# A two-layer relational GNN on one NeuronCore: the list of unseen edges built in smaller pieces

## The chip, the cores and the metric

One core of one Trainium2 chip. The metric is the device time of one execution in microseconds (us). The core has five engines that run side by side, each with its own queue of instructions in a fixed order: TensorE (PE, matmuls into the PSUM banks), VectorE (DVE), ScalarE (ACT), GpSimd (POOL, which issues the gathers) and SyncE (SP, which issues the other DMAs). They wait for one another through semaphores.

## The reference

A graph of 12,500 nodes with 128 features and 200,000 edges sorted by target. Every edge has one of 10 relations (the argmax of ten of its attributes). A layer averages the source features by target and relation, multiplies each average with the relation's matrix, and adds a root term and a bias. Two layers, a residual and a layer norm:

```python
def _rgcn_layer(x, src, dst, edge_type, w_rel, root, bias):
    seg = dst * NUM_REL + edge_type
    sums = segment_sum(x[src], seg, N * NUM_REL)
    cnt = segment_sum(ones, seg, N * NUM_REL)
    mean = (sums / maximum(cnt, 1.0)[:, None]).reshape(N, NUM_REL, -1)
    return einsum('nrd,rdo->no', mean, w_rel) + x @ root + bias

h = relu(_rgcn_layer(x, ..., w_rel1, root1, b1))
out = layernorm(x + _rgcn_layer(h, ..., w_rel2, root2, b2))
```

## The kernel before

A tile is 128 edges in target order; four tiles are a bunch. For each tile POOL gathers 128 rows of 512 bytes (L837), DVE makes a one-hot matrix of the targets with the edges' weights (`hots`, L844), PE multiplies the two into a PSUM bank, and DVE adds the result into the sums on chip. In the first layer (`layer_1`) the last part of the tiles also gathers those rows of the hidden features that are finished by then, so that a second layer's sum is made for a part of the edges on the way. The others are the unseen edges.

The second layer (`layer_2`) gathers rows of `YD`, the hidden features already multiplied with each relation's matrix. First come plain bunches, the tiles that saw no hidden features at all, in target order (`idxE`); then the unseen edges of the later tiles, from a compacted list (`idxB`, `keyB`, `wB`). The list is made while the plain bunches run, by `brought_together`, a Python generator: each `yield 1` ends a step, and the next step stands one bunch (four gathers) later in the program. What it does, on 127 partitions with 11 tiles' edges each:

- eleven rounds of a bitwise sort move the unseen edges of a partition to their slots (L1277 to L1289), in tiles named A, X, Y that lie one behind the other in `cc`;
- the sorting's last piece turns the keys round and zeroes the empty slots (L1292 to L1302): three instructions on 120 columns and three on 1416 (L1296, L1297, L1298), a copy by ScalarE (L1300), and two more (L1301, L1302). All this is one step. The keys end in `v`, three tile widths behind A, behind X and Y;
- `put` (L1307 to L1325), six times, collects 128 slots each. It makes indicators in X and Y in turn (L1318, L1320), multiplies them with the sorted edges (L1324; 12, 9, 7, 11, 4 and 10 products of 256 columns), and ScalarE copies the result to `packed` (L1325). The right side of a product is `both`, one access pattern over A and `v`;
- `listed` (L1329 to L1418) turns 128 packed slots into indices, keys and weights, in six steps; the first list's steps run in turn with the puts.

The order in the program is written out by hand. An iteration of `layer_2`'s loop, for bunch p, records: one-hots of bunch p + 3 (DVE), four gathers (POOL), four matmuls into one of three banks (PE, L1627), the next step of the list (`jobs.run`), then on DVE the sums of bunch p - 2 (L1657), which set that bank free for bunch p + 1; and, where a block of 256 nodes is complete, its normalisation: two transposes on PE (L1559) and L777 to L787 on DVE. A second list of due work, `between`, is looked at after every matmul of a bunch; the matmuls `alone` (L1540), which multiply the first layer's sums of the seen edges, stand there. Their data are loaded (L1533) once the first list is ready. There are 16 gather slots, that is four bunches: a bunch's gathers wait until PE has used those of four bunches before.

Of the kernel before, what the change touches and what calls it, by code (L numbers as in the profile page):

```python
# [9 lines left out]
F32 = mybir.dt.float32  # L10
BF16 = mybir.dt.bfloat16
I32 = mybir.dt.int32
AF = mybir.ActivationFunctionType
# [7 lines left out]
P = 128  # L21
# [8 lines left out]
QB = 4  # L30
# [11 lines left out]
YB = 512  # L42
# [28 lines left out]
def rgcn_resnorm_kernel(ctx: ExitStack, tc: tile.TileContext, x, src, dst, attr, w_rel1, root1, b1,  # L71
# [7 lines left out]
    nc = tc.nc  # L79
# [82 lines left out]
    for l, (a, last) in enumerate(((0, SPLIT), (SPLIT, NR))):  # L162
        while a < last:
            b = a + 1
# [9 lines left out]
            a = b  # L174
# [46 lines left out]
    ps_f = ctx.enter_context(tc.tile_pool(name="ps_f", bufs=2, space=PSUM))  # L221
# [140 lines left out]
    first = float(chunk_rows(NCH - 1) * P) - 0.5  # L362
# [55 lines left out]
    some = keep.tile([P, 1], F32, name="some")  # L418
# [723 lines left out]
    for a in range(0, NREL * RW, YB):  # L1142
        m = min(NREL * RW - a, YB)
# [37 lines left out]
    packed = comp.tile([P, -(-NT2 // P), 2 * P], F32, name="packed")  # L1181

    edge = STEP * (T0 + RT * SPLIT)

    def brought_together(ready, first):

        EW = P + ER
        spans_ = {}
# [73 lines left out]
        start = comp.tile([P, 4], I32, name="start")  # L1262
# [10 lines left out]
        for s in range(11):  # L1273
            m = 1 << s
# [10 lines left out]
            c = max(m, KW)  # L1285
# [8 lines left out]
        for a, b, t in ((0, KW, gl[:, :KW]), (KW, EW, go)):  # L1294
            q = t.bitcast(F32)
            nc.vector.tensor_scalar(t, d0[:, a:b], LOW - 1, None, op0=ALU.bitwise_and)  # L1296
            nc.vector.tensor_scalar(q, t, -1.0, high[:NR], op0=ALU.mult, op1=ALU.add)  # L1297
            nc.vector.scalar_tensor_tensor(v[:, a:b], d0[:, a:b], 0.5, q, op0=ALU.is_gt, op1=ALU.mult)  # L1298
        ga = go.bitcast(F32)
        nc.scalar.activation(ga, A[:, KW:], AF.Copy)  # L1300
        nc.vector.scalar_tensor_tensor(A[:, :KW], d0[:, :KW], 0.5, A[:, :KW], op0=ALU.is_gt, op1=ALU.mult)  # L1301
        nc.vector.scalar_tensor_tensor(A[:, KW:], d0[:, KW:], 0.5, ga, op0=ALU.is_gt, op1=ALU.mult)  # L1302
        yield 1
        n = -(-NT2 // P)
# [2 lines left out]
        both = bass.AP(A.tensor, A.offset, [A.ap[0], [far, 2], [1, EW]])  # L1307

        def put(i, c):

            u0, u1 = c * P, min(NT2, c * P + P) - 1
            p = u1 + 1 - u0
            m = max(-(-(P - 1 + cap_of[r]) // P) for r in range(rows_at(u0, extent[u0 >= UX])[0], rows_at(u1, extent[u1 >= UX])[1] + 1))
            assert m * P <= EW
            o = i * (EW // P)
            assert o + EW // P <= EW - KW
            qc = mask[:, o:o + EW // P].bitcast(F32)
            nc.vector.tensor_scalar(qc[:NR, :m], columns[:NR, :m], f[:NR, 3:4], -float(u0), op0=ALU.add, op1=ALU.add)  # L1318
            hot = hots[i % 2]
            nc.vector.tensor_tensor(hot[:, :m], columns[:NR, None, :].to_broadcast([NR, m, P]),  # L1320
                                    qc[:NR, :m, None].to_broadcast([NR, m, P]), op=ALU.is_equal)
            pp = ps_f.tile([P, YB], F32, name="pf")
            for j in range(m):
                nc.tensor.matmul(pp[:p, :2 * P], hot[:, j, :p], both[:, :, j * P:(j + 1) * P], start=(j == 0), stop=(j == m - 1))  # L1324
            nc.scalar.activation(packed[:p, c], pp[:p, :2 * P], AF.Copy)  # L1325

        put(0, first[0])
        yield 1
# [99 lines left out]
    def layer_2():  # L1428
# [51 lines left out]
        todo, jobs, between = Later(), Later(), Later()  # L1480
# [98 lines left out]
        used_ = {}  # L1579
        ready = set()  # L1580
        wanted = list(dict.fromkeys(c for second, t0, n, _ in bunches if second for c in (t0 // P, (t0 + n - 1) // P)))
        jobs.job(0, brought_together(ready, wanted), QB)
        made = i = ended = begins = 0
        opened = None
        for p in range(-AH, NB + BE):
# [21 lines left out]
            if p < NB:  # L1607
# [22 lines left out]
                i = issued[p + 1]  # L1630
# [204 lines left out]
```

## Time and profile before

| | |
|---|---|
| median of 3 runs | 3087.48 us (3087.31 to 3088.15) |
| the profiled execution, whole | 3085.23 us |
| its span, first to last instruction | 3083.4 us |
| POOL busy | 2289.6 us (74%) |
| PE busy | 2210.6 us (72%) |
| DVE busy | 1986.7 us (64%) |
| the list is built | about 2030 to 2195 us of the span, first list's slots from 2146 |

In a timeline row the first number is the start, the second the duration (of the whole group, where instructions in a row are merged), then engine, source line, operation, what it writes and reads, and how many; in brackets the idle time of the engine ahead of it and what ended it. `cc` is the large tile in which A, X, Y, `v` and the sums lie; `pf`, `zy`, `zq`, `go` are PSUM. The profile shows one float32 matmul of the source as two. A row of the windows view gives the window, its length, busy time of PE, weight loads, DVE, ACT and POOL, the granted PE clock (1.00 is full), the DMA share and GB/s.

### The profile page before, as it was taken

Reading aid. Unit: us, or ns where it says so; the run is one execution under the profiler, and the core shown is the slowest. Engines: PE = TensorE matmul, PEld = TensorE weight load, DVE = VectorE, ACT = ScalarE, POOL = GpSimd, SP = SyncE. Lnnn points to the kernel's source line nnn. Section 1 sums busy time; section 2 is a strip of 40 time slices with the busy share of each in tenths; the row PEclk is TensorE's granted clock in tenths of the full one; section 3 lists DMA queues with packets and bytes.
Section 4 is the critical chain, followed back from the end, with each engine's and each line's share of the span. In section 5 each row is a group of like instructions: output and inputs, shape, how many; then the busy total and the mean of one; then the engine's idle time right before and its main releaser. Section 6 shows DMA issues by size and latency. Waiting matters only on the chain. (4 is left out here: it accounts for less than half of the span.)

```text
span 3083.4 us, 37657 instructions
## 1 busy us (share of the span) xinstructions
PE 2210.6 (72%) x10645; PEld 1677.7 (54%) x10645; DVE 1986.7 (64%) x6410; ACT 511.5 (17%) x799; POOL 2289.6 (74%) x2430
## 2 busy tenths in 40 slices
PE   2768786878786878787778788644777767677554
PEld 1546575666565666566666666544544444444443
DVE  6867688978686858586767686488764334334332
ACT  2222222222222222221222221200000000000000
POOL 7777777777777777777777777676677777777775
PEclk7778888989898989998888889855778777777555
DMA  6655656666666666666666666621355454544222
GB/s 181 198 178 169 220 183 209 199 207 198 214 189 223 193 220 191 224 188 223 187 205 203 195 191 191 193 58 52 127 171 163 157 177 148 176 139 138 66 67 58
DMA packets 345316, 529.25 MB, mean 172 GB/s; under 512 B 55520, under 2 KB 225723, under 8 KB 345100
## 3 DMA queue, kind: packets, MB, share of 16 engines
q0 software_dynamic: 99552, 249.45, 28.4%
q1 hardware_dynamic: 218105, 264.48, 25.6%
q10 hardware_dynamic: 27443, 12.82, 1.4%
q8 instruction: 89, 1.46, 0.2%
q14 instruction: 127, 1.04, 0.1%
HBM read 372.75 MB, written 160.19 MB: 173 GB/s over the span
## 5 line engine op out<-in xcount | busy, mean ns | idle before, releaser
L837 POOL DMA_INDIRECT g<-XH,idxE x1386 | 1311.4, 946 | 430.3 <-issue 359.2
L1086 PE MATMUL zp<-oh,g 128*128 128x120 f32 x5898 | 944.8, 309 | 417.8 <-DVE cc L870 206.1
L1086 PEld LDWEIGHTS zp<-oh,g 128*128 128x128 f32 x5898 | 852.8, 216 | 629.8 <-DVE cc L870 353.5
L870 DVE TENSOR_TENSOR cc<-cc,zp 128x240 f32 (+1 forms) x1563 | 605.6, 387 | 430.8 <-PE zp L1086 279.9
L837 POOL DMA_INDIRECT g<-YD,idxB x678 | 640.9, 945 | 206.6 <-issue 191.9
L844 DVE TENSOR_SCALAR oh<-bank,keyE,wE 128x120 f32<-128x120 f32 x1563 | 517.3, 392 | 0.0
L1627 PE MATMUL zy<-oh,g 128*128 128x12 f32 (+30 forms) x1168 | 284.1, 358 | 231.1 <-DMA g<-YD,idxB 144.3
L1627 PEld LDWEIGHTS zy<-oh,g 128*128 128x128 f32 x1168 | 246.0, 273 | 353.8 <-DMA g<-YD,idxB 200.5
L944 ACT ACTIVATE ys<-yb 128x512 f32<-128x512 f32 (+2 forms) x291 | 152.9, 525 | 986.9 <-PE yb L938 691.7
L938 PE MATMUL yb<-w,a 128*128 128x512 f32 (+1 forms) x576 | 303.3, 613 | 5.5 <-ACT ys L944 5.5
L1540 PE MATMUL alone<-cc,w 128*128 128x512 f32 (+1 forms) x440 | 273.6, 708 | 0.0
L830 PE MATMUL pf<-cc,w 128*128 128x256 f32 (+2 forms) x1040 | 238.7, 388 | 6.3 <-DVE cc L870 5.9
L837 POOL DMA_INDIRECT g<-YD,idxE x177 | 168.0, 949 | 83.5 <-issue 59.8
L830 PEld LDWEIGHTS pf<-cc,w 128*128 128x128 f32 x1040 | 199.4, 204 | 36.5 <-issue 4.2
L1627 PE MATMUL zq<-oh,g 128*128 128x45 f32 (+33 forms) x542 | 138.2, 363 | 107.9 <-DMA g<-YD,idxB 106.5
L1627 PEld LDWEIGHTS zq<-oh,g 128*128 128x128 f32 x542 | 115.1, 261 | 182.8 <-DMA g<-YD,idxB 134.3
L799 ACT ACTIVATE cc<-zero 128x1280 f32<-128x1280 f32 x170 | 214.6, 1262 | 0.0
L777 DVE TENSOR_TENSOR cc<-pf,x 128x256 f32<-128x256 f32 (+2 forms) x52 | 21.2, 409 | 292.6 <-PE pf L1559 292.4
L837 POOL DMA_INDIRECT g<-in_x_dram,idxE x177 | 167.7, 947 | 55.6 <-issue 33.2
L844 DVE TENSOR_SCALAR oh<-columns,keyB,wB 128x45 f32<-128x45 f32 (+35 forms) x678 | 176.1, 335 | 0.0
L1657 DVE TENSOR_TENSOR cc<-cc,zy 128x12 f32 (+24 forms) x306 | 59.0, 193 | 116.5 <-PE zy L1627 95.6
L783 ACT ACTIVATE rstd<-mv,eps 128x2 f32<-128x2 f32 (+2 forms) x52 | 15.3, 295 | 682.9 <-DVE mv L781 682.8
(265 smaller groups left out, 1570.7 us busy)
## 6 DMA issues: line engine op xcount, KB each, us to landing
cc<-SD SPq DMA_DIRECT2D x21, 2560.0 KB
SD<-cc SPq DMA_DIRECT2D x41, 1280.0 KB
YD<-ys SPq DMA_DIRECT2D x194, 256.0 KB
m<-in_edge_attr_dram SPq DMA_DIRECT2D x48, 672.0 KB
g<-XH,idxE POOLq DMA_INDIRECT x1386
YD<-ys SPq DMA_DIRECT2D x97, 128.0 KB
XH<-hb SPq DMA_DIRECT2D x44, 256.0 KB
g<-YD,idxB POOLq DMA_INDIRECT x678
```

What stands on the lines that cost most here:

```text
L777: nc.vector.tensor_tensor(v[:p, s], pr[:p, s], xb[:p, s], op=ALU.add)
L799: nc.scalar.activation(cc[:, l, h * H:(h + 1) * H, o:o + n], zero[:, None, :n].to_broadcast([P, H, n]), AF.Copy)
L830: nc.tensor.matmul(po[:, :n], wsb[l][:, r, :], sums[:, r], start=(r == 0), stop=(w is None and r == NREL - 1))
L837: nc.gpsimd.indirect_dma_start(out=g[:, j * C:(j + n) * C], out_offset=None, in_=table, in_offset=bass.IndirectOffsetOnAxis(ap=idx, axis=0))
L844: nc.vector.tensor_scalar(oh[:, j * m:(j + 1) * m], cols[:, :m], keys[:, j:j + 1], weights[:, j:j + 1], op0=ALU.is_equal, op1=ALU.mult)
L870: nc.vector.tensor_tensor(s, s, z, op=ALU.add)
L938: nc.tensor.matmul(yb[:h, :m], fin_a[k][:, b * P:b * P + h], wsb[1][:, r:r + m // C, :], start=True, stop=True)
L944: nc.scalar.activation(ys[:h, :m], yb[:h, :m], AF.Copy)
L1086: nc.tensor.matmul(zp[:, o + l * KW:o + (l + 1) * KW], g[:, (slot[j] + l) * C:(slot[j] + l + 1) * C], oh[:, j * KW:(j + 1) * KW], start=Tr ...
L1540: nc.tensor.matmul(po[:, :n], wsb[1][:, r, :], sds[j][:, r, :n], start=(r == 0), stop=(r == NREL - 1))
L1627: nc.tensor.matmul(zp[:, o:o + w], g[:, at * C:(at + 1) * C], oh[:, j * w:(j + 1) * w], start=not second or j == 0, stop=not second or j = ...
L1657: nc.vector.tensor_tensor(s, s, zps[q][:, j * w:(j + 1) * w], op=ALU.add)
```

## The change

Two edits. The sorting's last piece gets two more `yield 1`: one between the second and the third instruction on 1416 columns, one ahead of L1302, so that it takes three steps, and every later step stands two bunches later. And `put` no longer issues its products itself: `spread` puts them into `between`, a quarter of them behind each of the four matmuls of the next bunch, the copy behind the last. The indicators stay in the step.

```diff
+            if a:
+                yield 1
             nc.vector.scalar_tensor_tensor(v[:, a:b], d0[:, a:b], 0.5, q, op0=ALU.is_gt, op1=ALU.mult)
         ga = go.bitcast(F32)
         nc.scalar.activation(ga, A[:, KW:], AF.Copy)
         nc.vector.scalar_tensor_tensor(A[:, :KW], d0[:, :KW], 0.5, A[:, :KW], op0=ALU.is_gt, op1=ALU.mult)
+        yield 1
         nc.vector.scalar_tensor_tensor(A[:, KW:], d0[:, KW:], 0.5, ga, op0=ALU.is_gt, op1=ALU.mult)
...
-            pp = ps_f.tile([P, YB], F32, name="pf")
-            for j in range(m):
-                nc.tensor.matmul(pp[:p, :2 * P], hot[:, j, :p], both[:, :, j * P:(j + 1) * P], start=(j == 0), stop=(j == m - 1))
-            nc.scalar.activation(packed[:p, c], pp[:p, :2 * P], AF.Copy)
+            held = []
+
+            def some(a, b):
+                if not a:
+                    held.append(ps_f.tile([P, YB], F32, name="pf"))
+                pp = held[0]
+                for j in range(a, b):
+                    nc.tensor.matmul(pp[:p, :2 * P], hot[:, j, :p], both[:, :, j * P:(j + 1) * P], start=(j == 0), stop=(j == m - 1))
+                if b == m:
+                    nc.scalar.activation(packed[:p, c], pp[:p, :2 * P], AF.Copy)
+            spread(m, some)
...
+        def spread(m, some):
+            for a in range(QB):
+                between.at(i + 1 + a, lambda _, a=a * m // QB, b=(a + 1) * m // QB: some(a, b))
+        jobs.job(0, brought_together(ready, wanted, spread), QB)
```

In the changed kernel lines 1298 to 1302 are 1300 to 1305, L1318 and L1320 are L1321 and L1323, L1324 is L1332, `listed`'s lines are 10 higher, L1627 is L1641 and L1657 is L1671.

DVE at the sorting's last piece, before; `oh_95` are the one-hots of a later bunch, `Z` and `go` scratch, `rowP` the table of places for the sums:

```order
L844 TENSOR_SCALAR oh_95<-columns,keyE,wE 128x12 x4
L1296 TENSOR_SCALAR Z<-cc 127x120
L1297 TENSOR_SCALAR Z<-Z,high 127x120
L1298 SCALAR_TENSOR_TENSOR cc<-cc,Z 127x120
L1296 TENSOR_SCALAR go<-cc 127x1416
L1297 TENSOR_SCALAR go<-go,high 127x1416
L1298 SCALAR_TENSOR_TENSOR cc<-cc,go 127x1416
L1301 SCALAR_TENSOR_TENSOR cc<-cc 127x120
L1302 SCALAR_TENSOR_TENSOR cc<-cc,go 127x1416
L855 TENSOR_LOAD rowP
```

All three wide instructions and the two of L1301 and L1302 stand ahead of the load with which the sums begin.

The same place in the changed kernel:

```order
L844 TENSOR_SCALAR oh_95<-columns,keyE,wE 128x12 x4
L1296 TENSOR_SCALAR Z<-cc 127x120
L1297 TENSOR_SCALAR Z<-Z,high 127x120
L1300 SCALAR_TENSOR_TENSOR cc<-cc,Z 127x120
L1296 TENSOR_SCALAR go<-cc 127x1416
L1297 TENSOR_SCALAR go<-go,high 127x1416
L855 TENSOR_LOAD rowP
L1671 ISA
L1671 TENSOR_TENSOR cc<-cc,zy_15678 128x12
```

The sums (L1671) now stand behind two of the three wide instructions; the other ones follow in the next two iterations.

PE from the first products on, before; `oh_94` is the bunch after them, L1359 and L1375 are `listed`'s first transposes, L1391 that of its second step:

```order
L1627 MATMUL zy_15678<-oh_93,g_89 128x12 x3
L1324 MATMUL pf<-cc 128x256 x12
L1559 MATMUL pf<-ident,cc 128x128 x2
L1627 MATMUL zy_15679<-oh_94,g_89 128x12 x4
L1324 MATMUL pf<-cc 128x256 x9
L1359 MATMUL pf<-ident,bs_f 128x128
L1375 MATMUL pf<-ident,bB 1x128
L1627 MATMUL zy_15680<-oh_95,g_89 128x12
L1627 MATMUL zy_15680<-oh_95,g_88 128x12 x3
L1324 MATMUL pf<-cc 128x256 x7
L1391 MATMUL pf<-ident,keyb 128x1
```

All products of a set stand between two bunches.

The same in the changed kernel, three bunches later (`oh_96`, `oh_97`):

```order
L1641 MATMUL zy_15678<-oh_96,g_88 128x12
L1332 MATMUL pf<-cc 128x256 x3
L1641 MATMUL zy_15678<-oh_96,g_88 128x12
L1332 MATMUL pf<-cc 128x256 x3
L1369 MATMUL pf<-ident,bs_f 128x128
L1385 MATMUL pf<-ident,bB 1x128
L1641 MATMUL zy_15679<-oh_97,g_88 128x12
L1332 MATMUL pf<-cc 128x256 x2
L1641 MATMUL zy_15679<-oh_97,g_89 128x12
```

The products stand inside the bunch, three behind each of its four matmuls, and the first list's transposes directly behind the last of them, ahead of the next bunch.

DVE in the changed kernel, the third set of indicators (896 columns), with what each waits for; its place between the one-hots and the sums is that of before:

```order
L844 TENSOR_SCALAR oh_93<-columns,keyE,wE 128x12 x4
L1321 TENSOR_SCALAR go<-columns,fB 127x7
L1323 TENSOR_TENSOR cc<-columns,go 127x896 [waits DVE_49,PE_49]
L1397 COPY keyb<-pf 1x2
L1399 TENSOR_REDUCE dn<-pf 1x31
L1400 COPY keyb<-dn 1x124 [waits DVE_49]
L1399 TENSOR_REDUCE dn<-pf 1x1 [waits DVE_49]
L1400 COPY keyb<-dn 1x2 [waits DVE_49]
L1402 TENSOR_SCALAR rowB<-keyb 1x128 [waits DVE_49]
L1671 ISA
L1671 TENSOR_TENSOR cc<-cc,zy_15680 128x12
```

The indicators wait for PE, and behind them in DVE's queue stand the list's step and the sums.

More of the change, by code (lines that the diff above doesn't have):

```diff
@@ L1183, in rgcn_resnorm_kernel, with brought_together @@
     edge = STEP * (T0 + RT * SPLIT)
-    def brought_together(ready, first):
+    def brought_together(ready, first, spread):
         EW = P + ER
@@ L1581, in layer_2 @@
         wanted = list(dict.fromkeys(c for second, t0, n, _ in bunches if second for c in (t0 // P, (t0 + n - 1) // P)))
-        jobs.job(0, brought_together(ready, wanted), QB)
+        def spread(m, some):
+            for a in range(QB):
+                between.at(i + 1 + a, lambda _, a=a * m // QB, b=(a + 1) * m // QB: some(a, b))
+        jobs.job(0, brought_together(ready, wanted, spread), QB)
         made = i = ended = begins = 0
```

## The prediction

> **What bounds the kernel now.** I read the chain that ended last first, then POOL's gathers by source line, then what POOL waited for, then the timeline around the list. The chain is POOL's gathers of the second layer. They come at an even pace, and from 2194 us to the last of them no pause is longer than 0.3 us, whatever ended it (the row of the most frequent kind):
>
> ```profile
> span 3083.4 us, 37657 instructions
> L837 POOL DMA_INDIRECT g<-YD,idxB x678: 940/945/1040, 2219.0 to 3065.2; - x170
> POOL g L837 <- issue: 197.1, 647, 0.3
> ```
>
> The pace is (3065.2 - 2219.0) / 677 = 1.25 us a gather, 5.0 us a bunch of four. So the end of the kernel moves by exactly what POOL pauses in excess of 0.30 before 2194 us. Where the list is built it pauses four times:
>
> ```profile
> 2144.19 0.95 POOL L837 DMA_INDIRECT g<-YD,idxE  x1 [0.30 <-issue]
> 2146.08 0.94 POOL L837 DMA_INDIRECT g<-YD,idxE  x1 [0.94 <-PE zy L1627]
> 2156.32 0.94 POOL L837 DMA_INDIRECT g<-YD,idxE  x1 [5.54 <-PE zy L1627]
> 2169.80 0.94 POOL L837 DMA_INDIRECT g<-YD,idxE  x1 [8.80 <-issue]
> 2192.72 0.94 POOL L837 DMA_INDIRECT g<-YD,idxE  x1 [3.21 <-PE zy L1627]
> ```
>
> That is 0.64 + 5.24 + 8.50 + 2.91 = 17.3 us lost. POOL has four bunches' worth of slots, so it stops when PE has not begun a bunch by the time POOL is four ahead; it goes on 0.6 to 0.9 us after that bunch's first matmul. The question is only: how long are the rounds from one bunch's first matmul to the next while the list is built?
>
> First pause, before:
>
> ```profile
> 2138.01 1.70 DVE L1297 TENSOR_SCALAR go<-go,high 127x1416 f32<-127x1416 int32 x1
> 2139.74 1.63 DVE L1298 SCALAR_TENSOR_TENSOR cc<-cc,go 127x1416 f32<-127x1416 int32 x1
> 2141.29 0.28 DVE L1301 SCALAR_TENSOR_TENSOR cc<-cc 127x120 f32<-127x120 int32 x1
> 2142.84 1.63 DVE L1302 SCALAR_TENSOR_TENSOR cc<-cc,go 127x1416 f32<-127x1416 int32 x1 [1.27 <-ACT go L1300]
> 2144.39 0.76 DVE L1657 TENSOR_TENSOR cc<-cc,zy 128x12 f32 x4
> 2145.07 0.88 DVE L844 TENSOR_SCALAR oh<-columns,keyE,wE 128x12 f32<-128x12 f32 x4
> 2145.21 1.88 PE L1627 MATMUL zy<-oh,g 128*128 128x12 f32 x8 [8.45 <-DVE cc L1657]
> 2146.11 1.75 DVE L1320 TENSOR_TENSOR cc<-columns,go 127x1536 f32<-127x1536 f32 x1
> 2147.79 0.56 DVE L1657 TENSOR_TENSOR cc<-cc,zy 128x12 f32 x3
> ```
>
> DVE's last sorting stretch ends at 2144.4; the sums (L1657) that free a PSUM bank stand behind it, and PE waits 8.45 us for them. A bunch starts 0.82 us after its sums (2144.39 to 2145.21).
>
> Then the products (L1324; one in the source is two matmuls here) and the indicators (L1320):
>
> ```profile
> 2147.97 7.73 PE L1324 MATMUL pf<-cc 127*128 127x256 f32 x24 [0.88 <-issue]
> 2155.53 0.38 PE L1559 MATMUL pf<-ident,cc 128*128 128x128 f32 x2
> 2155.95 0.42 DVE L777 TENSOR_TENSOR cc<-pf,x 128x256 f32<-128x256 f32 x1 [7.10 <-PE pf L1559]
> 2158.40 0.87 DVE L844 TENSOR_SCALAR oh<-columns,keyE,wE 128x12 f32<-128x12 f32 x4
> 2159.44 1.35 DVE L1320 TENSOR_TENSOR cc<-columns,go 127x1152 f32<-127x1152 f32 x1
> 2160.94 6.77 PE L1324 MATMUL pf<-cc 127*128 127x256 f32 x18 [4.23 <-DVE cc L1320]
> 2163.90 0.77 DVE L1657 TENSOR_TENSOR cc<-cc,zy 128x12 f32 x4 [0.57 <-issue]
> 2167.75 1.09 DVE L1320 TENSOR_TENSOR cc<-columns,go 127x896 f32<-127x896 f32 x1 [2.15 <-PE pf L1324]
> 2168.98 3.26 PE L1324 MATMUL pf<-cc 127*128 127x256 f32 x14 [0.26 <-DVE cc L1320]
> 2169.98 0.75 DVE L1657 TENSOR_TENSOR cc<-cc,zy 128x12 f32 x4
> 2172.28 1.62 DVE L1320 TENSOR_TENSOR cc<-columns,go 127x1408 f32<-127x1408 f32 x1 [0.62 <-PE pf L1324]
> 2174.05 4.99 PE L1324 MATMUL pf<-cc 127*128 127x256 f32 x22 [0.51 <-DVE bB L1394]
> 2174.85 0.77 DVE L1657 TENSOR_TENSOR cc<-cc,zy 128x12 f32 x4 [0.56 <-issue]
> 2176.62 0.69 DVE L1320 TENSOR_TENSOR cc<-columns,go 127x512 f32<-127x512 f32 x1
> 2182.55 0.76 DVE L1657 TENSOR_TENSOR cc<-cc,zy 128x12 f32 x4
> 2183.36 1.06 PE L1627 MATMUL zy<-oh,g 128*128 128x12 f32 x8 [1.42 <-DVE cc L1657]
> 2184.33 1.49 DVE L1320 TENSOR_TENSOR cc<-columns,go 127x1280 f32<-127x1280 f32 x1
> 2185.94 0.57 DVE L1657 TENSOR_TENSOR cc<-cc,zy 128x12 f32 x3
> 2185.97 6.24 PE L1324 MATMUL pf<-cc 127*128 127x256 f32 x20 [1.54 <-DVE cc L1320]
> ```
>
> The row to see is 2167.75. The third set of indicators is written into the tile that the first products read, and those ended near 2155.7. Yet it waits until 2167.7, when the second products end (2160.94 + 6.77); 2172.28 is the same, at the end of 2168.98 + 3.26. The products read their right side as one access that reaches from A to the sorted keys, with X and Y between them, so every set of indicators waits for all products of the set before. In before this costs DVE little, since PE ran those products while DVE did something else, ahead of the next bunch.
>
> **The change, part by part.** *The sorting's last piece.* Nothing is added. DVE now goes to its sums at 2138.01 + 1.70 = 2139.7, the next bunch starts at 2140.5 instead of 2145.2, and the 0.64 pause goes. The second piece (1.63 + 0.28) stands behind the sums (0.68 to the next L844) and an L844 (0.88) and ends near 2143.1; sums (0.76); then PE's two transposes (0.38) and the normalisation (2155.95 to 2158.40, 2.45) to 2146.8; L844 and the third piece (0.88 + 1.63) to 2149.3; sums (0.68); L844 and the first indicators (2145.07 to 2147.79, 2.72) to 2152.7; and 0.82 later, at 2153.5, the bunch that carries the first products starts. POOL is released at 2154.4. At its own pace POOL would reach the gather that waits for this bunch, three bunches after the one at 2146.08, at 2144.19 + 1.25 + 15.0 = 2160.4. So the split leaves POOL 6.0 us of room, and the two bunches by which the list comes later cost nothing: its first gather is at 2219.0, tens of us later.
>
> *The products.* The same 106 matmuls, the same six copies. But now they stand inside the next bunch, so one round is: bunch and products on PE, then (they wait for its end) the next indicators on DVE, the step of the list behind them, the sums, and only then the next bunch. Nothing of a round hides another part. Queued behind the waiting L1320 are the list's step, the sums and L844; PE waits for the sums, POOL for PE.
>
> DVE's part, from the start of L1320 to that of the sums, plus 0.82, from the rows above: 2159.44 to 2163.90, 5.28; 2167.75 to 2169.98, 3.05; 2172.28 to 2174.85, 3.39; 2176.62 to 2182.55, 6.75; 2184.33 to 2185.94, 2.43. After the last products two transposes (0.38) and one product with the root (two matmuls, 0.6 to 0.7 at a product's price below) stand on PE, 1.0. Sum 21.9.
>
> PE's part depends on the granted clock:
>
> ```profile
> 2174.00:2176.00 2.00, 1.95 (x9) 1.77 (x10) 1.34 (x8) 0.00 (x0) 1.45 (x2) 1.00 0.22 59
> 2188.00:2190.00 2.00, 2.00 (x6) 1.56 (x5) 0.00 (x0) 0.00 (x0) 1.21 (x2) 0.50 0.15 39
> ```
>
> A matmul took 0.23 where PE came from work at clock 1.00 (3.26 / 14, 4.99 / 22) and 0.32, 0.38 and 0.31 where it began at 0.50 after an idle wait (7.73 / 24, 6.77 / 18, 6.24 / 20). Now every round has such a wait, so I take 0.34, the mean of those three: 106 x 0.34 = 36.0. A bunch takes 1.06 to 1.88; six at 1.4 are 8.4.
>
> One by one the rounds are 14.9, 10.6, 9.6, 15.6, 6.5 and 9.2. Together 36.0 + 8.4 + 21.9 = 66.3 us, in which POOL alone would need 30.0; less the 6.0 of room, 30.3 are lost. The round after them holds the normalisation (2.45) and the second list's first step, from L844 to the next bunch:
>
> ```profile
> 2193.24 0.93 DVE L844 TENSOR_SCALAR oh<-columns,keyE,wE 128x12 f32<-128x12 f32 x4
> 2198.25 1.88 PE L1627 MATMUL zy<-oh,g 128*128 128x12 f32 x8 [1.07 <-DVE cc L1657]
> ```
>
> 5.0 + 2.45 - 5.0 = 2.4 more. Lost now 32.7, before 17.3: **15.4 us slower**. The profiled execution took 3085.23 in all, so 3100.6; the runs' median stood 2.25 above it, which gives 3103.
>
> Bounds of the unknown price: all matmuls at 0.23 and bunches at 1.0 take 11.7 + 2.4 off, +1.3 us; all at 0.40 (2.00 us for about five in a half-clock window) and 1.88 add 6.4 + 2.9, +24.7. That a product stands between two bunch matmuls costs nothing by itself, since each matmul loads its weights in either order.
>
> The Trainium skill, "TensorE: Matmul & The Clock Gate", section "HAM oscillation — how this bites in real kernels", says in its own words "no PE-idle gaps >~3.4µs". By it the waits of 3.05, 2.43 and 1.0 would leave the clock up. The trace speaks against it: before 2185.97 PE had been idle for 1.54, and the window at 2188 shows 0.50.
>
> **The rivals.** *The clock stays up over the shorter waits.* For: the products at 2174.05 kept 1.00 through a 0.51 wait. Against: the 0.50 at 2188. Then the sets of 14 and 20 matmuls cost 0.23: 34 x 0.11 = 3.7 less, +11.7, 3099. This is the skill's rule as a case; it changes the size, not the sign.
>
> *Full clock throughout.* If PE in small pieces is never idle long enough: +1.3, 3089, within what is called the same. Against it: six waits of 1 to 7 us.
>
> *The indicators wait only for the tile that they overwrite* (the other side). Two tiles in turn would let DVE write ahead, PE would run without gaps at 0.23, and the rounds would be 10.4 (24 x 0.23 + 1.0, then the first list step, which needs the first copy, 4.46 - 1.35 + 0.82), 5.1, 5.0, 6.1, 5.0 and 6.6 (5.0 where POOL's pace is longer): 38.2 - 30.0 - 6.0 + 2.4 = 4.6 lost, 12.7 us faster, 3075. It decides as soon as the second indicators start before the first products end. Against it: the row at 2167.75, and DVE's rows in the order, which keep a wait for PE.
>
> *The loads of the first layer's sums come too late.* They start when the last products have been read, tens of us later, and the second layer's matmuls that read them stand at fixed bunches; a few us on top, inside the range.
>
> **How the numbers follow.** Forecast of serial rounds 0.68; clock up over short waits 0.14; late loads on top 0.05; full clock 0.07; no wait 0.06. A measurement of this kernel can tell 0.2% (6.2 us) from no change. Slower by more: 0.68 + 0.14 + 0.05 = 0.87; same 0.07; faster 0.06. The range takes the price's bounds: from 3092 (a price of about 0.25) to 3114 (the upper bound, 3112, and 2 for late loads).
>
> **What would show it.** Right: the pause of 0.64 goes and the next lies after 2160; each set of indicators but the first (L1323 there) starts within 0.2 us of the end of the products before; the rounds are as listed; POOL pauses some 3.9, 5.6, 4.6, 10.6, 1.5, 4.2 and 2.4 us. Wrong: an L1323 that runs beside products of the set before; products at 0.23 with a granted clock of 1.00; or pauses after the list, where I have none.

## The result and the profile after

The changed kernel took 3094.4 us (median of 21 runs) against 3087.53 us for the kernel before; ratio 1.0020 with a 95% interval of 1.0014 to 1.0026, which is 4.3 to 8.0 us slower, 6.2 in the middle. One of the 21 runs, at 3159.69 us, is 2% slower than the others and left out of the ratio. The forecast was 3103, 15.4 us slower: the time lies in the range and the sign held, but the loss was forecast two and a half times too large.

The profiled execution took 3095.2 us in all, 9.97 more than that of before. Not all of it is the change. The same gather, ahead of any edited instruction, in the timeline of before and of after:

```profile
2038.34 0.94 POOL L837 DMA_INDIRECT g<-YD,idxE  x1 [0.30 <-PE zy L1627]
```

```profile
2043.57 0.94 POOL L837 DMA_INDIRECT g<-YD,idxE  x1 [0.30 <-PE zy L1641]
```

After was 5.23 us late before it met the edit; such differences come and go between executions (the 21 runs of the kernel before lie between 3080.28 and 3093.3 us). The pauses of POOL leave them out, so I compare by those. POOL's pauses in the changed kernel (timeline, gathers alone, those idle for over 0.33 us while the list is built; the number in brackets is the idle time, of which 0.30 is the usual pace):

```profile
2173.43 0.94 POOL L837 DMA_INDIRECT g<-YD,idxE  x1 [3.06 <-PE zy L1641]
2183.66 0.94 POOL L837 DMA_INDIRECT g<-YD,idxE  x1 [5.55 <-PE zy L1641]
2193.17 0.94 POOL L837 DMA_INDIRECT g<-YD,idxE  x1 [4.82 <-PE zy L1641]
2201.41 0.94 POOL L837 DMA_INDIRECT g<-YD,idxE  x1 [3.56 <-PE zy L1641]
2207.75 0.94 POOL L837 DMA_INDIRECT g<-YD,idxE  x1 [1.65 <-PE zy L1641]
2215.82 0.94 POOL L837 DMA_INDIRECT g<-YD,idxE  x1 [3.38 <-PE zy L1641]
2222.61 0.94 POOL L837 DMA_INDIRECT g<-YD,idxE  x1 [2.08 <-PE zy L1641]
2248.06 0.94 POOL L837 DMA_INDIRECT g<-YD,idxB  x1 [0.74 <-PE zy L1641]
```

The excess over 0.30 is 2.76, 5.25, 4.52, 3.26, 1.35, 3.08, 1.78 and 0.44, in sum 22.4 us. Before it was 17.3. The 5.1 us between them lie inside the measured 4.3 to 8.0. The pause of 0.64 is gone, as foreseen; long pauses in fewer places became shorter ones at every round.

The indicators (L1323) and the products (L1332) around them, in the timeline of the changed kernel:

```profile
2165.77 1.54 PE L1332 MATMUL pf<-cc 127*128 127x256 f32 x6
2167.34 1.35 DVE L1323 TENSOR_TENSOR cc<-columns,go 127x1152 f32<-127x1152 f32 x1 [8.11 <-PE pf L1332]
2172.56 0.60 PE L1641 MATMUL zy<-oh,g 128*128 128x12 f32 x2 [0.97 <-DVE cc L1671]
2178.39 1.54 PE L1332 MATMUL pf<-cc 127*128 127x256 f32 x6
2179.96 1.09 DVE L1323 TENSOR_TENSOR cc<-columns,go 127x896 f32<-127x896 f32 x1 [6.54 <-PE pf L1332]
2192.30 0.60 PE L1641 MATMUL zy<-oh,g 128*128 128x12 f32 x2 [3.44 <-DVE cc L1671]
2192.75 2.05 PE L1332 MATMUL pf<-cc 127*128 127x256 f32 x4
2193.20 0.69 DVE L1323 TENSOR_TENSOR cc<-columns,go 127x512 f32<-127x512 f32 x1
2199.14 0.76 DVE L1671 TENSOR_TENSOR cc<-cc,zy 128x12 f32 x4
2199.36 1.54 PE L1332 MATMUL pf<-cc 127*128 127x256 f32 x6
2200.85 0.29 PE L1641 MATMUL zy<-oh,g 128*128 128x12 f32 x2
```

The second set starts 0.03 us after the first products end (2165.77 + 1.54 = 2167.31), the third 0.03 after the second (2178.39 + 1.54). The fifth, at 2193.20, doesn't wait: it starts 0.45 us after the fourth products begin, and 7.7 before they end (2199.36 + 1.54 = 2200.90). So DVE reaches its sums at 2199.14, while PE still has products to do, and the next bunch starts at 2200.85 without waiting. The row at 2193.20 is the one in which the forecast was wrong.

### The profile page after: what moved, and what is told of

Read it like the earlier page. It is cut to its first block, busy times and chain, and to the rows that moved or that the text cites. A ratio compares the mean times of both kernels' runs of the same rounds, so it can differ in the third digit from the quotient of the medians.

```text
span 3093.3 us, 37650 instructions
## 1 busy us (share of the span) xinstructions
PE 2212.8 (72%) x10645; PEld 1678.8 (54%) x10645; DVE 1988.0 (64%) x6410; ACT 510.7 (17%) x799; POOL 2287.9 (74%) x2430
## 5 line engine op out<-in xcount | busy, mean ns | idle before, releaser
L1641 PE MATMUL zy<-oh,g 128*128 128x12 f32 (+30 forms) x1168 | 285.3, 356 | 234.5 <-DMA g<-YD,idxB 144.1
L1641 PEld LDWEIGHTS zy<-oh,g 128*128 128x128 f32 x1168 | 250.3, 275 | 361.2 <-DMA g<-YD,idxB 203.1
L777 DVE TENSOR_TENSOR cc<-pf,x 128x256 f32<-128x256 f32 (+2 forms) x52 | 21.2, 409 | 287.6 <-PE pf L1569 287.4
L1641 PEld LDWEIGHTS zq<-oh,g 128*128 128x128 f32 x542 | 112.3, 257 | 165.8 <-DMA g<-YD,idxB 118.9
L1641 PE MATMUL zq<-oh,g 128*128 128x45 f32 (+33 forms) x542 | 134.5, 359 | 94.0 <-DMA g<-YD,idxB 91.0
L1671 DVE TENSOR_TENSOR cc<-cc,zy 128x12 f32 (+24 forms) x306 | 58.5, 191 | 117.2 <-PE zy L1641 98.2
L783 ACT ACTIVATE rstd<-mv,eps 128x2 f32<-128x2 f32 (+2 forms) x52 | 15.3, 295 | 668.9 <-DVE mv L781 668.8
```

The costliest lines, as they stand in the source:

```text
L777: nc.vector.tensor_tensor(v[:p, s], pr[:p, s], xb[:p, s], op=ALU.add)
L1641: nc.tensor.matmul(zp[:, o:o + w], g[:, at * C:(at + 1) * C], oh[:, j * w:(j + 1) * w], start=not second or j == 0, stop=not second or j = ...
L1671: nc.vector.tensor_tensor(s, s, zps[q][:, j * w:(j + 1) * w], op=ALU.add)
```

## The experiments

Each kernel ran beside the kernel before on the same chip. The table has POOL's pauses while the list is built, in the profiled execution, and the ratio of the times.

| kernel | pauses, us | against 17.3 | ratio to before, 95% interval | in us |
|---|---|---|---|---|
| changed kernel | 22.4 | +5.1 | 1.0020 (1.0014 to 1.0026) | +6.2 |
| the same, another chip | 23.0 | +5.7 | 1.0017 (1.0008 to 1.0026) | +5.2 |
| first edit alone | 6.8 | -10.5 | 0.9963 (0.9949 to 0.9977) | -11.4 |
| second edit alone | 25.3 | +8.0 | 1.0017 (1.0007 to 1.0027) | +5.2 |
| changed, fifth set waits | 32.6 | +15.3 | 1.0061 (1.0047 to 1.0074) | +18.8 |
| changed, pieces | 7.8 | -9.5 | 0.9968 (0.9956 to 0.9979) | -9.9 |
| the same, another chip | 7.3 | -10.0 | 0.9976 (0.9964 to 0.9988) | -7.4 |
| changed, clock kept up | 21.5 | +4.2 | 1.0011 (1.0001 to 1.0020) | +3.4 |
| changed, pieces, list later | 4.6 | -12.7 | 0.9955 (0.9942 to 0.9969) | -13.9 |
| the same, long step cut | 0 | -17.3 | 0.9960 (0.9945 to 0.9975) | -12.3 |
| products ahead, pieces, list later | 0 | -17.3 | 0.9946 (0.9934 to 0.9959) | -16.7 |

In ten of the eleven rows the difference of the pauses lies inside the interval of the time; the exception is the cut of the long step (-17.3 against -17.0 at the interval's end). So the time follows the pauses, as far as these intervals, 4 to 9 us wide, can tell.

**One edit at a time.** The kernel before with the first edit alone:

```diff
             nc.vector.tensor_scalar(q, t, -1.0, high[:NR], op0=ALU.mult, op1=ALU.add)
+            if a:
+                yield 1
...
+        yield 1
         nc.vector.scalar_tensor_tensor(A[:, KW:], d0[:, KW:], 0.5, ga, op0=ALU.is_gt, op1=ALU.mult)
```

> The kernel before with the first edit alone: the sorting's last piece in three steps, all products of a set still ahead of the next bunch. Theory (the split gives POOL 6.0 us of room ahead of the products, and POOL's pauses set the end): the pauses of 0.64 and 5.24 go, those at the third products and the last (8.50 and 2.91) stay, sum 11.4 instead of 17.3, so some 5.9 us faster than before. Rival (the room is lost again at the next wait, since the list comes two bunches later): pauses of 17 in sum, within 1 us of before.

Its pauses, in the timeline of POOL, and the second products, in that of PE:

```profile
2167.27 0.94 POOL L837 DMA_INDIRECT g<-YD,idxE  x1 [0.54 <-PE zy L1630]
2172.80 0.94 POOL L837 DMA_INDIRECT g<-YD,idxE  x1 [0.84 <-PE zy L1630]
2179.09 0.94 POOL L837 DMA_INDIRECT g<-YD,idxE  x1 [1.60 <-PE zy L1630]
2193.79 0.94 POOL L837 DMA_INDIRECT g<-YD,idxE  x1 [5.02 <-PE zy L1630]
```

```profile
2162.50 4.15 PE L1327 MATMUL pf<-cc 127*128 127x256 f32 x18 [0.65 <-DVE cc L1323]
```

The room came, and the pauses are 10.5 us shorter, 4.6 more than the expected 5.9: the pause of 8.50 has gone too. Before, a normalisation stood between the first products and the second indicators; PE idled 4.23 us and the second products took 6.77. With the list two bunches later the normalisation falls into the sorting, PE idles 0.65 and the same 18 matmuls take 4.15. The first edit is a gain of 11 us, and the 4.6 of it that I did not foresee are luck: they come from where the normalisation happens to fall.

The second edit alone, the changed kernel without the two `yield 1`:

> The second edit alone: products spread behind the matmuls of a bunch, the sorting's last piece in one step. Theory: the pauses of the changed kernel (22.4 us) and the 6.0 us of room that it lacks, some 28 to 29 us of pauses, so 11 to 12 us slower than before, 6 slower than the changed kernel. Rival (the split does nothing here): as the changed kernel, 5 slower than before.

Pauses of 25.3, about 3 less than expected: here the normalisations (L777) start at 2160.78, beside the first products, and at 2220.86, behind the last, so that none lengthens a round. The time came out as the rival had it, but its interval (2.2 to 8.3 us) takes in the 8.0 of the pauses as well. By the pauses, spreading adds 8.0 us to the kernel before and 15.6 to the kernel with the first edit (22.4 - 6.8).

**The waits.** The indicators in instructions of at most 512 columns:

```diff
-            nc.vector.tensor_tensor(hot[:, :m], columns[:NR, None, :].to_broadcast([NR, m, P]),
-                                    qc[:NR, :m, None].to_broadcast([NR, m, P]), op=ALU.is_equal)
+            for a in range(0, m, 4):
+                z = min(m, a + 4)
+                nc.vector.tensor_tensor(hot[:, a:z], columns[:NR, None, :].to_broadcast([NR, z - a, P]),
+                                        qc[:NR, a:z, None].to_broadcast([NR, z - a, P]), op=ALU.is_equal)
```

In the trace of that kernel no piece waits for the products of the set directly before it. The one wait for products, 1.68 us ahead of the fourth set's second piece, ends at 2176.03, when the second products, which read the same tile, are almost done.

> The changed kernel with each set of indicators written in instructions of at most 512 columns (three for 12 blocks), so that no set waits for the products of the set directly before it, only for those that read its own tile two sets before. Theory (the rounds are long because DVE waits for the products, then PE for DVE): every set but the first starts within 0.5 us of the one-hots ahead of it; the first round stays near 13 us, since the list's first step needs the first copy, the other five fall to 5 to 8 us; pauses 8 us or less in sum instead of 22.4, 14 us faster than the changed kernel, 9 faster than before. Rival (the half granted clock of the products is what makes the rounds long): the rounds shorten by no more than the indicators' own 1 to 1.6 us each, 6 us in sum.

> The changed kernel with indicators in pieces of at most 512 columns, beside the changed kernel on one chip. Theory (each set waits for all products of the one before): 14 us faster than the changed kernel where the engines don't stand still, 8 to 14 where they do. Rival: 6 or less.

Timeline of that kernel, DVE from the second set on (a row stands for the whole group; the first group is all three pieces):

```profile
2155.93 1.48 DVE L1325 TENSOR_TENSOR cc<-columns,go 127x512 f32<-127x512 f32 x3
2164.56 0.23 DVE L1360 CAST li<-packed 128x128 int32<-128x128 f32 x1 [7.15 <-ACT packed L1336]
2167.78 0.77 DVE L1673 TENSOR_TENSOR cc<-cc,zy 128x12 f32 x4 [0.57 <-PE pf L1387]
```

The second set is written beside the first products. DVE now waits for something else, the first copy that the list's first step reads (7.15 us), and the sums still stand behind it: the first round keeps 13.6 us. The second took 8.1, the others 4.0 to 6.4, and the pauses fell from 22.4 to 7.8 as expected (7.3 in the other run). In time the gain was 12.6 us on the chip on which the changed kernel ran beside it (+5.2 and -7.4), where 14 were expected. These 15 us of pauses are what the indicators' waits cost, with what they do to the clock: from the third set on, six products now take 1.54 us each time.

The opposite: the fifth set written over 896 columns, three blocks of which nothing reads, so that it waits as the others do.

```diff
-            nc.vector.tensor_scalar(qc[:NR, :m], columns[:NR, :m], f[:NR, 3:4], -float(u0), op0=ALU.add, op1=ALU.add)
+            nc.vector.tensor_scalar(qc[:NR, :max(m, 7)], columns[:NR, :max(m, 7)], f[:NR, 3:4], -float(u0), op0=ALU.add, op1=ALU.add)
             hot = hots[i % 2]
+            w = max(m, 7)
-            nc.vector.tensor_tensor(hot[:, :m], columns[:NR, None, :].to_broadcast([NR, m, P]),
-                                    qc[:NR, :m, None].to_broadcast([NR, m, P]), op=ALU.is_equal)
+            nc.vector.tensor_tensor(hot[:, :w], columns[:NR, None, :].to_broadcast([NR, w, P]),
+                                    qc[:NR, :w, None].to_broadcast([NR, w, P]), op=ALU.is_equal)
```

> The changed kernel with the fifth set's indicators written over 896 columns instead of 512 (three blocks that nothing reads), which makes them wait for the fourth set's products as the others do. It costs 0.4 us of DVE by itself. Theory (my forecast was too high because the fifth set alone doesn't wait, so that the 6.75 us of the list's third step run beside the fourth products): the round behind the fourth products goes from 8.55 to 15 us, POOL pauses 6 to 7 us longer, 6 to 7 us slower than the changed kernel. Rival (the step of the list runs beside them anyway, or the products' price was the error): within 1 us of the changed kernel.

The fifth set and the bunch behind it, in the timeline of that kernel:

```profile
2187.12 0.60 PE L1642 MATMUL zy<-oh,g 128*128 128x12 f32 x2 [3.44 <-DVE cc L1672]
2195.71 1.09 DVE L1324 TENSOR_TENSOR cc<-columns,go 127x896 f32<-127x896 f32 x1 [7.72 <-PE pf L1333]
2201.97 0.76 DVE L1672 TENSOR_TENSOR cc<-cc,zy 128x12 f32 x4
2202.79 0.60 PE L1642 MATMUL zy<-oh,g 128*128 128x12 f32 x2 [6.32 <-DVE cc L1672]
```

The fourth round is 15.7 us (2202.79 - 2187.12), where the forecast had 15.6 and the changed kernel 8.55; 0.4 of the difference is the wider set's own work (1.09 us instead of 0.69). The pauses are 32.6 in sum, the forecast's 32.7 (one by one they differ: 10.7 of it, as forecast, at the fourth round, 2.2 more than forecast at the fifth, 1.1 less at the first). With the wait that I had supposed, the fourth round is the one that I forecast; that the sums agree so closely is in part luck. And it is more than this run's own expectation, 6 to 7 us of pauses on top of the changed kernel's 22.4: it was 10.2. PE idles 6.32 us ahead of the fifth products there, each pair of them takes 1.07 us where the changed kernel has 0.62, and the fifth round is 8.7 us instead of 6.2.

**The clock.** Products of which nothing is read fill PE's idle time behind the sets:

```diff
                 if b == m:
                     nc.scalar.activation(packed[:p, c], pp[:p, :2 * P], AF.Copy)
+                    for _ in range((6, 4, 5, 0, 4, 0)[i]):
+                        nc.tensor.matmul(pp[:, 2 * P:4 * P], wsb[1][:, 0, :], wsb[1][:, 0:2, :], start=True, stop=True)
```

> The changed kernel with 6, 4, 5, 0 and 4 extra products behind the first five sets, beside the changed kernel on one chip. Theory (half clock after PE's idle time): all products together 32 us or less instead of 38, POOL's pauses 5 to 7 us less, the time 5 to 7 us less than the changed kernel's. Rival (the extra products delay the next bunch by as much as they shorten the products): within 2 us of the changed kernel.

The windows of 2 us at the third set of the changed kernel, then two at the third set of this one and one at its fifth (the granted clock is the third number from the end), and rows of this one's PE timeline:

```profile
2182.00:2184.00 2.00, 1.38 (x9) 1.24 (x10) 1.75 (x10) 0.00 (x0) 0.34 (x1) 1.00 0.03 8
2184.00:2186.00 2.00, 2.00 (x8) 1.69 (x8) 0.00 (x0) 0.00 (x0) 1.55 (x2) 0.54 0.12 33
2186.00:2188.00 2.00, 2.00 (x7) 1.66 (x8) 0.00 (x0) 0.00 (x0) 1.53 (x2) 0.61 0.20 57
```

```profile
2174.00:2176.00 2.00, 1.71 (x11) 1.55 (x11) 1.43 (x8) 0.00 (x0) 0.70 (x1) 1.00 0.00 0
2176.00:2178.00 2.00, 2.00 (x12) 1.81 (x12) 0.00 (x0) 0.00 (x0) 1.39 (x3) 1.00 0.12 33
2192.00:2194.00 2.00, 2.00 (x6) 0.71 (x4) 0.00 (x0) 0.00 (x0) 1.70 (x2) 0.50 0.23 66
```

```profile
2183.59 1.54 PE L1332 MATMUL pf<-cc 127*128 127x256 f32 x6
2189.97 0.39 PE L1643 MATMUL zy<-oh,g 128*128 128x12 f32 x2 [1.69 <-DVE cc L1673]
2196.31 3.78 PE L1336 MATMUL pf<-w 128*128 128x256 f32 x8 [0.47 <-ACT packed L1334]
```

Where the fillers did their work, in the third and fourth sets, the clock stayed at 1.00. Four product matmuls took 1.11 us there and six 1.54, so each further one 0.215, as in the kernel before (3.26 for 14, 4.99 for 22: 0.216): their place inside the bunch costs them nothing. A row of a few matmuls has a larger mean only because some 0.24 us at its end are shared by fewer (6 x 0.215 + 0.25 = 1.54, 14 x 0.216 + 0.24 = 3.26). All 106 matmuls together took 38.1 us in the changed kernel (groups by line) and 29.7 in the kernel with the cut, below, which spreads them in the same way with the clock up most of the time. The first four pauses fell from 16.3 to 13.0 us (both on this chip). But PE idled 1.69 us ahead of the fifth set, the clock was at 0.50, and the fillers there took 3.78 us and gave it back (5.18 of pause where the changed kernel has 1.36). In sum 1.5 us of pauses less than the changed kernel on this chip (23.0), where 5 to 7 were expected, and no difference in time that the intervals can tell; all 106 product matmuls took 34.4 us, where 32 or less were expected. The number is the rival's, while the clock rose and the products went faster as the theory had it, in the sets that the fillers reached in time.

**What is left.** To the pieces I added the list's steps one bunch later:

```diff
             put(i + 1, c)
-            next(head, None)
+            if i:
+                next(head, None)
             yield 1
```

> Pieces, and the first list's steps one bunch later, beside the pieces alone on one chip. Theory (DVE's wait for the first copy makes the first round long): the first round 9 or 10 us instead of 13.6, 3 to 4 us faster than the pieces alone. Rival (the step only moves to a round that is then longer): within 1 us.

The next lines are its only pause, in POOL's timeline, and what stands ahead of it on PE and DVE:

```profile
2194.04 0.94 POOL L837 DMA_INDIRECT g<-YD,idxE  x1 [4.94 <-PE zy L1644]
```

```profile
2182.61 0.77 DVE L1674 TENSOR_TENSOR cc<-cc,zy 128x12 f32 x4 [0.56 <-issue]
2183.43 0.60 PE L1644 MATMUL zy<-oh,g 128*128 128x12 f32 x2 [2.69 <-DVE cc L1674]
2186.01 2.90 PE L1334 MATMUL pf<-cc 127*128 127x256 f32 x6
```

The first round is 9.1 us (2152.15 to 2161.21 for the bunches) and POOL no longer pauses there; the theory holds for the round. The pauses fell by 2.6 us on that chip (7.3 to 4.6), where 3 to 4 us were expected; the times, -7.4 and -13.9, can't tell more. What stays is the long step of the list on DVE, behind which the sums begin at 2182.61: PE idles 2.69 us and its products run at half clock (2.90 for six). The last two kernels went at that. One cuts the step in two:

```diff
         nc.vector.tensor_tensor(fl[:p], fl[:p], b[:p, 1:2], op=ALU.max)
+        yield 1
         nc.vector.tensor_scalar(li[:p], li[:p], P - 1, None, op0=ALU.bitwise_and)
```

> The fastest so far (the changed kernel, indicators in pieces, the list one bunch later), with one more step: the list's longest step on DVE (6.75 us in the kernel before) is cut in two behind its check of the widths. Theory (the one pause left, 4.64 us, comes from that step, behind which the sums stand while PE idles 2.69 us and falls to half clock for the sixth products): the pause goes to 0 to 2 us, 3 us faster than without it, 16 to 17 faster than before. Rival (the sixth products at half clock come from their place and stay): within 1 us of it.

The other has all of this but the cut and the spreading: the sorting in three, the products ahead of the bunch as before, pieces, the list one bunch later.

> The same without the spreading and without the cut: sorting in three, products ahead of the bunch, indicators in pieces, the list's steps one bunch later. Theory (once DVE waits for no products, it makes little difference where they stand; the sums behind the long step still wait): pauses 3 to 6 us, 11 to 15 us faster than before, within 3 us of the spread kernel with the same pieces and steps. Rival (spread products cover DVE's steps better): 5 or more slower than that.

POOL's gathers from 2130 to 2290 us of the second one, by line, and its second, fourth and sixth products in PE's timeline:

```profile
L837 POOL DMA_INDIRECT g<-YD,idxE x63 | 59.5, 944 | 19.2 <-issue 15.8 <-DMA g<-YD,idxE 1.5 <-PE zy L1633 1.2
```

```profile
2165.36 4.13 PE L1329 MATMUL pf<-cc 127*128 127x256 f32 x18
2174.28 5.00 PE L1329 MATMUL pf<-cc 127*128 127x256 f32 x22
2183.26 4.56 PE L1329 MATMUL pf<-cc 127*128 127x256 f32 x20
```

63 gathers idle 19.2 us, 0.30 each: no pause, where I had expected 3 to 6 us. The same holds for the cut, where 0 to 2 were expected. These sets run at 0.23 us a matmul (4.13 / 18, 5.00 / 22, 4.56 / 20). Both kernels beat the one before, 3071.04 and 3073.3 us beside 3086.22, and the two intervals overlap. The cut gained nothing that the times show (-12.3, against -13.9 without it on another chip), though its pauses are gone; the 16 to 17 us expected of it are not shown. Once DVE waits for no products of the set before, the spreading gains nothing that the times show (-16.7 without it, -13.9 and -12.3 with it).

**Runs that told less.** Four of these kernels ran first on two other chips, where all engines stood still together for some 3 us again and again and the kernel before took 3682.05 and 3679.76 us; these ratios are not comparable with the others.

> The sorting's last piece in three, each set's products ahead of the next bunch as in the kernel before, and the indicators in instructions of at most 512 columns. Theory (what is left in the sorting alone, pauses of 6.8 us, is mostly the last products, which wait for all 1280 columns of their indicators and then run at half clock, 7.29 us): the products start when the first 512 columns are written, 0.9 to 1.2 us earlier in each set, and the sixth set keeps the full clock; pauses 3 to 4 us, 3 us faster than the sorting alone, 14 faster than before. Rival (no set waits for the set before it when the products stand ahead of the bunch, so that pieces only add instructions to DVE): within 1 us of the sorting alone.

> The changed kernel with indicators in pieces of at most 512 columns, and the first list's steps one bunch later, so that no step of the list stands directly behind the products that it reads. Theory (the one long round left is the first, 13.6 us, in which DVE waits for the first products' copy and PE then for DVE): that round falls to 9 or 10 us, POOL's pauses from 7.8 to 3 or 4, 4 us faster than with the pieces alone. Rival (the list's step costs the same wherever it stands, PE's products at half clock set the round): within 1 us of it.

> The sorting's last piece in three, products ahead of the bunch, indicators in pieces, and the first list's steps one bunch later. Theory: without the step behind the first copy the second round shortens by up to 3 us, but POOL hardly pauses there any more (0.24 and 0.54 with the sorting alone), so only 0 to 2 us faster than the same kernel with the steps where they were. Rival (DVE's queue is what sets the pace): 3 or more.

> The changed kernel with 6, 4, 5, 0 and 4 extra products of 256 columns behind the first five sets (their result is not read, they write a part of the bank that nothing uses), which fill PE's idle time before the next bunch. Theory (a product costs 0.36 us instead of 0.234 because PE idles between the sets and the granted clock falls to 0.50): the windows of the later sets show 1.00, their products 0.23 to 0.26, POOL's pauses fall from 22.4 to 12 to 15 us, 7 to 10 us faster than the changed kernel. Rival (products between bunch matmuls are slow by themselves, weight loads and changes of bank): the price stays at 0.34 to 0.36, and the time is the changed kernel's or 1 to 3 us more.

> The kernel of the sorting in three, products ahead of the bunch and indicators in pieces, once more, since in the run before all engines of that chip stood still together for some 3 us again and again and every kernel took 19% longer there. Theory: without those stops POOL's pauses are 3 to 4 us instead of the 6.8 of the sorting alone, since the sixth products start earlier and at the full clock; 13 to 14 us faster than before. Rival: as the sorting alone, 10 to 11 us faster than before.

> The changed kernel with indicators in pieces and the first list's steps one bunch later, once more. Theory (DVE's wait for the first products' copy makes the first round 13.6 us): the round falls to 9 or 10 us, pauses 3 to 4 instead of 7.8, 13 to 14 us faster than before. Rival (the step costs the same wherever it stands): 10 us faster than before, as with the pieces alone.

> The sorting in three, products ahead of the bunch, indicators in pieces and the list's steps one bunch later, once more. Theory: 0 to 2 us faster than the same with the steps where they were, since POOL hardly pauses in the first rounds any more. Rival (DVE's queue sets the pace there): 3 or more.

> The changed kernel with 6, 4, 5, 0 and 4 extra products behind the first five sets, whose result is not read, once more. Theory (the half clock after PE's idle time makes a product cost 0.36 us instead of 0.234): later sets' windows at 1.00, products 0.23 to 0.26 us, POOL's pauses 12 to 15 us instead of 22.4, 7 to 10 us faster than the changed kernel, about as before or up to 3 faster. Rival (products between bunch matmuls are slow by themselves): the changed kernel's time or 1 to 3 us more.

The sorting with products ahead and pieces gave 0.9975 (0.9964 to 0.9986) and 0.9979 (0.9966 to 0.9992); with the list later 0.9980 (0.9969 to 0.9991) and 0.9975 (0.9962 to 0.9989), no difference. Spread, with pieces and the list later, gave 0.9996 (0.9986 to 1.0006) and 1.0000 (0.9988 to 1.0012), the clock kept up 1.0013 (1.0004 to 1.0022) and 0.9996 (0.9984 to 1.0009). So there the kernel with products ahead and the list later kept about half of its gain, and the spread one lost all of its; why was not tried. Without the changed kernel beside them they settle nothing, and three of the four were made again as above. The first, without the list one later, was not.

The changed kernel itself once more, on the chip of the fillers and of the list one bunch later:

> The changed kernel itself, as the base of the three runs beside it. Theory (its loss is the waits of POOL while the list is built, 22.4 us instead of 17.3): 5 to 7 us slower than before where the engines don't stand still; where they do, the same sign, but less sure, since POOL's room is then used up by the stops as well. Rival (the loss seen so far is chance of the first layer): within 2 us of before.

It repeated: 23.0 us of pauses, 2.5 to 8.0 us slower.

## Why the prediction was right in sign and more than twice too large

**What bounds the kernel.** Right. In the table the time follows POOL's pauses while the list is built, in ten rows of eleven.

**The sorting's last piece.** The 6.0 us of room held: the round of the first products was 14.2 us (2158.36 to 2172.56 for the bunches), POOL needs 5.0 and paused 2.76, so it had 6.4 in hand.

**The products' price.** I took 0.34; 106 matmuls took 38.1 us in the groups of L1332, 0.36 each. But these rows overlap with the bunch's own (one ends at 2165.79, 2164.25 + 1.54, and the bunch's next matmuls start at 2165.62), so they don't add up to the time of a round. From a bunch's first matmul to the end of its last product, PE's timeline has 9.0, 7.4, 5.9, 8.6, 3.8 and 7.2 us, 41.7 in sum, where I had 36.0 + 8.4 = 44.4: PE's part was 2.7 us too large. DVE's parts came out as I had them, 5.25, 3.07, 3.44 and 2.47 for 5.28, 3.05, 3.39 and 2.43, but for the one that never came, 6.75. The rival of full clock throughout is out, and so is the one by which the clock stays up over short waits: ahead of the third set PE idled 2.11 and 0.58 us (PE's timeline of the changed kernel), and the windows quoted above show 0.54 and 0.61 from 2184 on:

```profile
2182.04 0.38 PE L1401 MATMUL pf<-ident,keyb 1*128 1x1 f32 x2 [2.11 <-DVE keyb L1400]
2183.00 0.39 PE L1641 MATMUL zy<-oh,g 128*128 128x12 f32 x2 [0.58 <-DVE cc L1671]
```

The Trainium skill, "TensorE: Matmul & The Clock Gate", section "HAM oscillation — how this bites in real kernels", names PE idle gaps over about 3.4 us as what lowers the clock. Here the clock fell after gaps of 2.11 and 0.58 us, and the measurement decides.

**The rounds.** The step that failed is one sentence: "Nothing of a round hides another part." It holds for the rounds in which the next indicators wait, forecast 14.9, 10.6, 9.6, 6.5 and 9.2, measured 14.2, 10.4, 9.3, 6.2 and 8.2. For the fourth I forecast 15.6 and it was 8.55. The fifth set, 512 columns, doesn't wait for the fourth products, so DVE went through the list's longest step (6.75 us with the start of the bunch) beside them, and the round is PE's part alone. That is 7.1 us of round and 7.3 of the 10.3 us by which the pauses were forecast too long; the rest is 0.1 to 1.1 us in each other round (3.4 in sum), less a pause of 0.44 that I had not foreseen, at 2248.06.

The evidence stood in my own rows. The indicators at 2176.62 start before the fourth products end (2174.05 + 4.99 = 2179.04), in the same fence as the row at 2167.75 on which I built the rule. I took from 2167.75 that the products' access from A to the sorted keys makes every set wait. The kernels show the other half of it: the sets of 1152, 896, 1408 and 1280 columns wait, that of 512 doesn't, 896 columns make it wait, and pieces of at most 512 free all of them. The products of the set before read nothing that the indicators write, so the wait comes from the program as compiled, and it depends on how many blocks one instruction writes. Where between 4 and 7 blocks it begins was not tried. What in the compiler decides it is not shown, and neither is my reason for it, the one access from A to the sorted keys: it would hold for 512 columns as well, and no kernel reads the two parts apart.

**The rivals.** "The indicators wait only for the tile that they overwrite" had 0.06 and came true for one set of five. With all five freed it is the run with pieces, 7.8 us of pauses where I had 4.6 lost; I had the first round at 10.4, and it is 13.6 in that run, since I let the first products run at full clock. The late loads are at most the pause of 0.44.

**What neither edit's price showed.** The forecast set the two edits against before as a whole, and so missed that they pull apart: the first alone takes 10.5 us of pauses away, the second puts 15.6 on top.

## What to carry to other kernels

A wait read from one row is not a rule until every other instance of the same instruction has been held against it; the exception is worth as much as the rule. Before moving work so that it stands between a wait and its release, ask what of the round will still run side by side. And price the parts of a change apart: a gain and a loss in one diff look like a small effect.

## What the runs showed of the chip

In the changed kernel the granted clock fell at 2184 with PE idle for 2.11 us or less at a time since 2172.56, and in the kernel with the fillers it was 0.64 and 0.50 from 2166 on, after idle times of 0.47, 0.37 and 1.07 us. It rose late: in the changed kernel's first round dense work begins at 2158.4, and the windows of 2 us show 0.50 at 2160 and 1.00 at 2164. Over the stretch of the products (2158 to 2216) it was 0.77; in the kernel with the cut, which has no pauses, 0.93 (2152 to 2192):

```profile
2160.00:2162.00 2.00, 2.00 (x8) 1.64 (x7) 0.00 (x0) 0.00 (x0) 1.39 (x3) 0.50 0.14 37
2164.00:2166.00 2.00, 2.00 (x13) 1.82 (x12) 0.00 (x0) 0.00 (x0) 1.39 (x3) 1.00 0.13 33
2158.00:2216.00 58.00, 44.46 (x172) 35.11 (x172) 25.58 (x108) 2.39 (x7) 28.52 (x31) 0.77 0.13 35
```

```profile
2152.00:2192.00 40.00, 34.66 (x173) 28.34 (x172) 29.18 (x125) 2.95 (x8) 30.19 (x32) 0.93 0.19 53
```

And on two of the chips all engines stood still together for some 3 us at a time; whether that is the chip or the hour is not shown. Such a stop in the timeline, of the kernel with products ahead and pieces: nothing starts on any engine between 2597.00 and 2601.62.

```profile
2597.00 0.94 POOL L837 DMA_INDIRECT g<-YD,idxE  x1 [0.30 <-issue]
2601.62 0.42 DVE L777 TENSOR_TENSOR cc<-pf,x 128x256 f32<-128x256 f32 x1 [11.14 <-remote]
```

POOL's gathers of the first layer idled 805.0 us there, where they idled 430.3 in before on the first chip, at the same 0.95 us of work each (groups by line; before first):

```profile
L837 POOL DMA_INDIRECT g<-XH,idxE x1386 | 1311.4, 946 | 430.3 <-issue 359.2 <-PE zp L1086 29.1 <-DMA g<-XH,idxE 11.9
```

```profile
L837 POOL DMA_INDIRECT g<-XH,idxE x1386 | 1310.0, 945 | 805.0 <-issue 366.0 <-PE zp L1086 211.0 <-remote 179.9
```
